# One attention norm of a gated-scan and Hadamard-FFN kernel moved earlier and sent through memory

## The chip, the cores and the metric

The kernel runs on one core of a Trainium2 chip. The core has five engines that work beside each other, each from its own queue in order: TensorE (PE in the profile, with PEld for its weight loads), VectorE (DVE), ScalarE (ACT), GpSimd (POOL) and SyncE (SP), which here only issues DMAs. POOL issues DMAs too: its stores stand in its queue between its few arithmetic instructions. The metric is the device time of one execution in microseconds; the median of the runs shown is compared. Everything is computed in float32.

## The reference

Four sequences of 512 rows and 512 columns go through an attention layer and a feed-forward layer, each behind a layer norm, with a residual sum of the normalized output:

```python
x = x + _layernorm(_L0_attn_ref(_layernorm(x), Wi, Wf, Wg, Wo, gnorm_w))
x = x + _layernorm(_L0_ffn_ref(_layernorm(x), W1, W2, W3))

# attention: i, f, g = x Wi^T, x Wf^T, x Wg^T
gate = sigmoid(f); v = silu(i) * (1 - gate)
o_t = gate_t * o_(t-1) + v_t                 # a scan over the 512 rows
o = o * rsqrt(mean(o * o) + EPS) * gnorm_w * g * sigmoid(g)
out = o Wo^T

# feed-forward: hidden = silu(x W1^T) * (x W3^T), 2048 wide
out = fwht(hidden) W2^T                      # Walsh-Hadamard transform of each row
```

The Hadamard transform of `hidden` is done on W2 instead, once, at the start of the kernel.

## The kernel before

**Products.** Each large product is done with seven block products in place of eight. Both sides are cut into 2x2 blocks; VectorE makes four combinations of each side (`combine_left`, `combine_right`: S1 to S4 and T1 to T4), and `seven` (L445) runs the products in the order P1, P2, P6, P5, P7, P3, P4. P1, P6 and P5 are first copied out of PSUM by ScalarE (L470), P2, P7 and P3 are added by VectorE (L468), and P4 closes with a copy or a sum. Two products share one PSUM bank (X: P1, P6, P7, P4), so P6 may start when the copy of P1 has read the bank, P7 when that of P6 has, and P4 when the sum of P7 has.

**Units.** An attention layer of a sequence b is three units of seven products: `attn_unit(b, 0)` and `attn_unit(b, 1)` give two halves of i and f and, behind P4, the gates and the scan; `attn_unit(b, 2)` gives g and the gated output `og`. The scan of a unit is cut in two: the first half directly behind the gates (`scan(0)`, L523), the second during the next unit, behind its P7 (`second`, put into `beside` at step 4). `attn_out(b)` is the product with Wo: its seven steps are put into the list `fill` and taken out one by one between the products of the following units. The feed-forward layer has eight units for each sequence and four partial output products.

**The norm and the transpose.** A unit's right side is the normalized x, transposed. `normalize_tiles` (L251) takes the statistics of two row tiles on VectorE, the power -1/2 on POOL (L244), and applies scale and bias on ScalarE (L289), tile by tile. From there two ways lead on. For sequences 0 and 1 of the attention layer (`ON_TENSOR`, L249), `transposes` uses TensorE with an identity into four PSUM banks (`pt`, L386), and VectorE and ScalarE copy the result out. For all others ScalarE writes the columns in a folded order, POOL stores the tile to memory (L298), SP loads it back in 32-row pieces (`load_fold`, L418, eight DMAs of 128 KB), and VectorE's 32x32 stream transpose finishes it (`transpose_fold`, L436, two steps of four instructions and then `combine_right`).

**Order.** The orders of TensorE and SP are those of the program text. VectorE, ScalarE and POOL are ordered by a planner by priority; `tc.high_priority(offset=...)` moves work forward (URGENT is 400, SOON 200) and `behind(what)` keeps it behind a named instruction, such as the read of P7 of the current unit. `beside[k]` holds work to be made after product k of the next unit. `acts` and `sums` hold small steps of the output norms; `pace` says how many of `sums` are released after P2, P7 and P3. FULL, SLOW and NONE are three such paces.

**Start of the kernel.** In the first 70 us, sequence 0 runs its three attention units; the w2 matrix is transformed between their products (`transform_high` on TensorE, L742, `butterfly_a` and `butterfly_b` on VectorE, L747 to L761, stores by POOL); the combined weights are stored (`kept`, L161) so that later sequences reload them with one DMA each (`again`, L168). The statistics of sequence 1's norm stand behind unit (0,1) on VectorE; the norm is applied in unit (0,2), and the TensorE transposes stand at the end of it. `load_wo` and `prepare_wo` (L697 and L708) load Wo, scale it by gnorm and combine it; both halves are prepared in one step after P2 of unit (0,2). In SP's queue `load_wo` is followed at once by the reloads of wi and wf for unit (1,0).

Of the kernel before, what the change touches and what calls it, by code (L numbers as in the profile page):

```python
# [44 lines left out]
def kernel(  # L45
# [50 lines left out]
    def slot():  # L96
# [8 lines left out]
    pace = {}  # L105
    FULL, SLOW, NONE = (
        {"P2": a, "P7": b, "P3": c} 
        for a, b, c in ((1, 1, 3), (0, 1, 2), (0, 0, 0))
    )
    pace.update(FULL)  # L110

# [28 lines left out]
    def combine_left(t, eng, steps=(0, 1)):  # L140

        if 0 in steps:
            eng.tensor_add(t[:, S1], t[:, A21], t[:, A22])
            eng.tensor_sub(t[:, S2], t[:, S1], t[:, A11])
        if 1 not in steps:
            return
        eng.tensor_sub(t[:, S3], t[:, A11], t[:, A21])
        return eng.tensor_sub(t[:, S4], t[:, A12], t[:, S2])
# [40 lines left out]
    def combine_weights(n=None, steps=(0, 1)):  # L189
        for _ in range(len(uncombined) if n is None else n):  # L190
            key, t = uncombined.pop(0)
            read["combined"] = combine_left(t, nc.vector, steps)
            if 1 in steps:
                kept(key, t)
            else:
                uncombined.append((key, t))
# [33 lines left out]
    def behind(what):  # L230


        return tc.issue_after(read[what].ins)
# [12 lines left out]

    xns, xnd = {}, {}

    ON_TENSOR = ("a", 0), ("a", 1)  # L249

    def normalize_tiles(b, name, i0, n, later=False):  # L251

        if (name, b) not in xns:
            xns[name, b] = work.tile(  # L260
                [P, NT, D], F32, tag="wide", name=f"xn_{name}_{b}", bufs=3
            )
        t = xns[name, b]
        st = small.tile([P, n, 6], F32, tag=f"st{n}", name=f"st_{name}_{b}_{i0}")
        mv = small.tile([P, n, 2], F32, tag=f"mv{n}", name=f"mv_{name}_{b}_{i0}")
        for k in range(n):
            nc.vector.bn_stats(st[:, k, :], xs[b][:, i0 + k, :])
            nc.vector.bn_aggr(mv[:, k, :], st[:, k, :])
        r = inverse_root(mv, EPS, f"{name}_{b}_{i0}")
        nb = small.tile([P, n], F32, tag="nb", name=f"nb_{name}_{b}_{i0}", bufs=8)  # L270

        def bias():

            read["nb"] = nc.vector.scalar_tensor_tensor(
                nb, mv[:, :, 0], -1.0, r, ALU.mult, ALU.mult
            )

        if later != "bias":
            bias()

        def apply(tiles=range(n)):
            if later == "bias":
                bias()
            for k in tiles:
                x_t, to = xs[b][:, i0 + k, :], t[:, i0 + k, :]
                if (name, b) not in ON_TENSOR:
                    x_t = x_t.rearrange("p (i a c) -> p i c a", c=ND, a=32)
                    to = to.rearrange("p (i c a) -> p i c a", c=ND, a=32)
                read["xn"] = nc.scalar.activation(  # L289
                    to, x_t, AF.Identity, bias=nb[:, k : k + 1], scale=r[:, k : k + 1]  # L290
                )
            if (name, b) not in ON_TENSOR:
                if (name, b) not in xnd:
                    xnd[name, b] = scratch.tile(
                        [NT, P, D], F32, tag=f"xn_{name}_{b}", name=f"xnd_{name}_{b}"
                    )
                if tiles[-1] == n - 1:
                    nc.gpsimd.dma_start(  # L298
                        out=xnd[name, b][i0 : i0 + n].rearrange("t p d -> p t d"),
                        in_=t[:, i0 : i0 + n, :],  # L300
                    )

        if later:
            return apply
        apply()
# [193 lines left out]
    def into_left(t, a, b2, c=None):  # L499

        to = t[:, 0:4] if c is None else t[:, 0:4, c]
        nc.vector.tensor_mul(  # L502
            to.rearrange("p (t k) f -> p k t f", t=2),
            a.rearrange("p k (t f) -> p k t f", t=2),
            b2.rearrange("p k (t f) -> p k t f", t=2),
        )
# [4 lines left out]
    def attn_unit(b, u, dense=False):  # L511
        def gates(d):

            v, gate = d[:, 0], d[:, 1]
            nc.scalar.activation(gate, gate, AF.Tanh, scale=0.5)
            nc.scalar.activation(v, v, AF.Silu)
            nc.vector.scalar_tensor_tensor(v, gate, 1.0, v, ALU.subtract, ALU.mult)
            nc.scalar.activation(gate, gate, AF.Identity, bias=half_t, scale=0.5)
            if u == 0:
                os_[b] = work.tile([P, 2, 2, T], F32, tag="o", name=f"o_{b}")  # L520

            def scan(h):
                nc.vector.tensor_tensor_scan(  # L523
                    os_[b][:, u, h, :], gate[:, h, :], v[:, h, :], 0.0, ALU.mult, ALU.add
                )

            def second():
                with behind("P7"):
                    scan(1)

            scan(0)
            beside.setdefault(4, []).append(second)

        def output_gate(d):
            o = os_[b]
            og = work.tile([P, 7, 2, H], F32, tag="og", name=f"og_{b}")
            for m in range(2):
                nc.scalar.activation(d[:, m], d[:, m], AF.Silu)
                into_left(og, o[:, m], d[:, m], m)
            combine_left(og, nc.vector)  # L540
            ogs[b] = og

            def square(m):
                nc.scalar.activation(o[:, m], o[:, m], AF.Square)
                if m:
                    nc.vector.tensor_add(o[:, 0], o[:, 0], o[:, 1])
                    nc.vector.tensor_add(o[:, 0, 0], o[:, 0, 0], o[:, 0, 1])

            acts.insert(1, partial(square, 1))
            acts.appendleft(partial(square, 0))  # L550

        project(
            attn_w.pop((b, u)), xts["a", b], f"a_{b}_{u}", gates if u < 2 else output_gate,
            dense,
        )
# [149 lines left out]
                )  # L705
        return w

    def prepare_wo(w):  # L708
        for c in range(2):
            for k, blocks in enumerate(((B11, B12), (B21, B22))):  # L710
                t = w[c][:, blocks[0] : blocks[1] + 1 : blocks[1] - blocks[0]]
                g = gn_sb[:, 2 * k + c : 2 * k + c + 1]
                nc.vector.tensor_scalar(t, t, g, -1.0, ALU.mult, ALU.mult)
            combine_right(w[c], nc.vector)
            kept(("wo", c), w[c])
# [29 lines left out]
    def butterfly_a(g):  # L745

        x, y = w2_p[2 * g], w2_p[2 * g + 1]  # L747
        nc.vector.tensor_add(x[:, 2], x[:, 0], y[:, 0])
        nc.vector.tensor_sub(y[:, 0], x[:, 0], y[:, 0])
        nc.vector.tensor_add(x[:, 0], x[:, 1], y[:, 1])  # L750
        nc.vector.tensor_sub(y[:, 1], x[:, 1], y[:, 1])
# [109 lines left out]

    fill.extend([second_half] + high(2, NJ))
    attn_unit(0, 0, True)
    with behind("P2"):
        combine_weights(2)
        for g in range(2):
            butterfly_a(g)
            butterfly_b(g)
    attn_unit(0, 1)
    with behind("P3"):  # L870
        with tc.high_priority(offset=URGENT):
            combine_weights(2)
        with tc.high_priority(offset=SOON):
            apply = [normalize_tiles(1, "a", i, 2, True) for i in (0, 2)]
    with behind("P2"):
        butterfly_a(2)
    wo_t[0] = load_wo()
    load_attn_w(1, 0)
    while fill:
        slot()  # L880

    def wo_behind_sum():
        with behind("P2"):
            prepare_wo(wo_t[0])

    def behind_copy(*makes):
        with behind("copy"):
            for make in makes:
                make()

    fill.extend([wo_behind_sum, partial(behind_copy, *apply)] + transposes(1, "a"))
    attn_unit(0, 2)
    load_x(2)
    load_attn_w(1, 1)
# [1 line left out]
    def beside_copies(b, places):  # L896
# [2 lines left out]
            late = [normalize_tiles(b, "a", i, 2, True) for i in (0, 2)]  # L899
        for t, place in enumerate(places):  # L900
            yield place, partial(behind_copy, partial(late[t // 2], range(t % 2, t % 2 + 1)))

    def transpose_beside(b, name, places=((1, "P2"), (4, "P7"), (6, "P3"))):


        def step(make, what):
            with behind(what), tc.high_priority(offset=SOON):
                make()

        for make, (k, what) in zip(transpose_fold(b, name), places):  # L910
            beside.setdefault(k, []).append(partial(step, make, what))

    fill.extend([None] * 3 + attn_out(0))
    attn_unit(1, 0, True)
# [7 lines left out]
    pace.update(SLOW)  # L922
    attn_unit(1, 2)
    pace.update(FULL)
    load_attn_w(2, 1)
    fill.extend([None] * 3 + attn_out(1))
    for k, what, make, g in (
# [7 lines left out]
        transpose_beside(0, "f", ((6, "P3"), (7, "P2"), (8, "P7")))  # L935

    beside.setdefault(2, []).append(fold_beside)
    attn_unit(2, 1, True)
    load_ffn_w(0, 0)
    load_low(0)  # L940
# [2 lines left out]
    pace.update(NONE)  # L943
    attn_unit(2, 2)
    pace.update(SLOW)
    with behind("P7"), tc.high_priority(offset=SOON):
        combine_weights()

    LOW = {1: (0, "combined", 0), 3: (1, "P2", 2), 5: (2, "P2", 2), 6: (3, "P2", 2)}

# [92 lines left out]
```

## Time and profile before

| | |
|---|---|
| median of 3 runs | 817.80 us (817.74 to 818.98) |
| the profiled execution's own time | 817.91 us |
| its span, first to last instruction | 816.1 us |
| TensorE busy | 802.0 us (98%), mean granted clock 0.995 |
| VectorE, ScalarE, POOL busy | 492.7 (60%), 265.6 (33%), 68.0 (8%) us |
| DMA | 160.62 MB, mean 197 GB/s |

A time line gives the start in microseconds from the span's start, the duration, the engine, the line of the source, the operation, the tiles (out<-in) and shapes, and in brackets the idle time of that engine before it and what ended it. `d_a` is the projection of an attention unit, `d_f` that of a feed-forward unit, `xt` the transposed right side, `og` the gated output, `y` the attention's output. A list of waits gives who waited for whom, the total, the count and the longest. DMA lines give size and time from issue to landing; SPq and POOLq are the queues that issue.

### The profile page before, as it was taken

The numbers are of one execution on the slowest core, as the hardware profiler recorded it, in microseconds if no ns is written. First come the engines' busy times: TensorE is split into PE (matmuls) and PEld (weight loads), VectorE is DVE, ScalarE is ACT, GpSimd is POOL, SyncE is SP. The second block draws the span as 40 slices with busy tenths as digits, with TensorE's granted clock in tenths as the row PEclk, the third lists the DMA queues.
The fourth block names the chain that finished last, engine by engine and source line by source line (L and its number), as shares of the span: only waits on it lengthen the run. The fifth ranks groups of instructions, "written<-read, shape, count | busy, mean of one in ns | idle before, by whom it ended". The sixth has DMA issues, their size and how long they took to land.

```text
span 816.1 us, 9850 instructions
## 1 busy us (share of the span) xinstructions
PE 802.0 (98%) x3704; PEld 698.6 (86%) x3704; DVE 492.7 (60%) x1002; ACT 265.6 (33%) x376; POOL 68.0 (8%) x105
## 2 busy tenths in 40 slices
PE   9999999999999999999999999999999999999995
PEld 7788878888888888888888888888888888888884
DVE  6998599799778874455335448645433534544345
ACT  4564654444442221123311233323432111331111
POOL 2120102011211000011000000101000000100000
PEclk9999999999999999999999999999999999999998
DMA  9995355676777883444654354726373442534201
GB/s 332 408 352 211 113 217 209 179 259 213 282 274 288 277 300 139 185 162 192 248 157 173 139 163 162 270 94 233 115 249 130 186 181 91 204 156 188 88 4 51
DMA packets 66415, 160.62 MB, mean 197 GB/s; under 512 B 4800, under 2 KB 40256, under 8 KB 66368
## 3 DMA queue, kind: packets, MB, share of 16 engines
q1 hardware_dynamic: 57168, 115.69, 40.6%
q0 software_dynamic: 8480, 43.00, 13.3%
q10 hardware_dynamic: 720, 1.31, 0.4%
q8 instruction: 29, 0.48, 0.2%
q14 instruction: 18, 0.15, 0.1%
HBM read 115.94 MB, written 44.04 MB: 196 GB/s over the span
## 4 chain that ended last, share of the span: by engine, by line
PE 94%; DVE 4%; ACT 0%; issue 0%; POOL 0%; POOLq 0%; DVEq 0%; ACTq 0%
PE X_f L487 27%; PE Z_f L487 14%; PE X_po L645 13%; PE X_a L487 9%; PE Z_po L645 7%; PE Y_f L487 6%; PE Z_a L487 4%; PE X_y L587 3%; PE Y_po L645 3%; PE Y_a L487 2%; PE Z_y L587 2%; PE h L742 2%; PE Y_y L587 1%; PE warm L818 1%; DVE o L523 0%; PE pt_a L386 0%
## 5 line engine op out<-in xcount | busy, mean ns | idle before, releaser
L487 PE MATMUL X_f<-xt_f,w 128*128 128x256 f32 x1024 | 242.1, 379 | 1.2 <-ACT d_f L470 1.2
L487 PEld LDWEIGHTS X_f<-xt_f,w 128*128 128x128 f32 x1024 | 194.2, 190 | 28.2 <-ACT d_f L470 2.0
L470 ACT COPY d_f<-X_f 128x512 f32<-128x512 f32 x96 | 56.3, 586 | 331.7 <-PE X_f L487 294.2
L645 PE MATMUL X_po<-w,ht 128*128 128x256 f32 x512 | 120.9, 379 | 0.2 <-DVE f L468 0.2
L487 PE MATMUL Z_f<-xt_f,w 128*128 128x256 f32 x512 | 121.0, 379 | 0.0
L645 PEld LDWEIGHTS X_po<-w,ht 128*128 128x128 f32 x512 | 97.2, 190 | 13.8 <-DVE f L468 0.6
L487 PEld LDWEIGHTS Z_f<-xt_f,w 128*128 128x128 f32 x512 | 97.3, 190 | 13.2
L468 DVE TENSOR_TENSOR f<-X_po,f 128x512 f32<-128x512 f32 x51 | 35.1, 688 | 93.8 <-PE X_po L645 93.7
L502 DVE TENSOR_TENSOR ht<-d_f 128x1024 f32<-128x1024 f32 x32 | 39.2, 1224 | 61.7 <-ACT d_f L621 46.9
L645 PE MATMUL Z_po<-w,ht 128*128 128x256 f32 x256 | 60.5, 379 | 0.0
L487 PE MATMUL Y_f<-xt_f,w 128*128 128x256 f32 x256 | 60.5, 379 | 0.0
L487 PEld LDWEIGHTS Y_f<-xt_f,w 128*128 128x128 f32 x256 | 48.6, 190 | 6.6
L645 PEld LDWEIGHTS Z_po<-w,ht 128*128 128x128 f32 x256 | 48.6, 190 | 6.6
L468 DVE TENSOR_TENSOR d_f<-X_f,d_f 128x512 f32<-128x512 f32 x32 | 22.1, 690 | 50.9 <-PE X_f L487 43.3
L244 POOL TENSOR_TENSOR rs_f<-rs_f,power 128x2 f32<-128x2 f32 x16 | 14.4, 900 | 401.1 <-DVE nm_f L345 347.1
L470 ACT COPY d_a<-X_a 128x512 f32<-128x512 f32 x36 | 21.1, 585 | 69.8 <-PE X_a L487 67.3
L487 PE MATMUL X_a<-xt_a,wi 128*128 128x256 f32 x128 | 33.3, 382 | 1.1 <-ACT d_a L470 1.0
L621 ACT ACTIVATE d_f<-d_f 128x1024 f32<-128x1024 f32 x32 | 33.8, 1057 | 1.0
L487 PE MATMUL X_a<-xt_a,wf 128*128 128x256 f32 x128 | 32.8, 379 | 0.0
L468 DVE TENSOR_TENSOR d_f<-Z_f,d_f 128x512 f32<-128x512 f32 x32 | 21.9, 685 | 16.4 <-PE Z_f L487 16.4
L487 PEld LDWEIGHTS X_a<-xt_a,wi 128*128 128x128 f32 x128 | 23.9, 190 | 8.9 <-issue 2.9
L468 DVE TENSOR_TENSOR f<-Z_po,f 128x512 f32<-128x512 f32 x28 | 19.3, 688 | 20.1 <-PE Z_po L645 20.1
(161 smaller groups left out, 1023.9 us busy)
## 6 DMA issues: line engine op xcount, KB each, us to landing
w<-s_w SPq DMA_DIRECT2D x72, 896.0 KB, 6.0
s_w<-w POOLq DMA_DIRECT2D x24, 896.0 KB, 6.4
w<-in_W_dram SPq DMA_DIRECT2D x32, 256.0 KB, 5.9
wi<-s_wi SPq DMA_DIRECT2D x6, 896.0 KB, 9.5
wf<-s_wf SPq DMA_DIRECT2D x6, 896.0 KB, 8.1
wg<-s_wg SPq DMA_DIRECT2D x6, 896.0 KB, 5.5
w_h<-w2p POOLq DMA_DIRECT2D x8, 512.0 KB, 7.6
xnd_f<-xn_f POOLq DMA_DIRECT2D x8, 512.0 KB, 5.1
```

Source lines behind the costliest of these rows:

```text
L244: read["power"] = nc.gpsimd.tensor_tensor(r, r, power_t[:, 0:n], ALU.pow)
L468: read[what] = nc.vector.tensor_add(to, ps[which], to)
L470: read["copy"] = nc.scalar.copy(to, ps[which])
L487: nc.tensor.matmul(ps[:, n, :], w[:, a, c, :], xt[:, bb, c, :], start=first and n == 0 and c == 0, stop=c == 1, skip_group_check=True,)
L502: nc.vector.tensor_mul(to.rearrange("p (t k) f -> p k t f", t=2), a.rearrange("p k (t f) -> p k t f", t=2), b2.rearrange("p k (t f) -> p k ...
L587: nc.tensor.matmul(ps[:, t, :], og[:, a, c, ts(t, P)], w[c][:, bb, :], start=first and t == 0 and c == 0, stop=c == 1, skip_group_check=True,)
L621: nc.scalar.activation(d[:, 0], d[:, 0], AF.Silu)
L645: nc.tensor.matmul(ps[:, t, :], hts[b, m][:, a, ts(t, P)], w[m][:, W2[bb], :], start=first and t == 0 and m == ms[0], stop=m == ms[-1], sk ...
L742: nc.tensor.matmul(p, h_sb, t[:, k, :], start=True, stop=True)
L818: nc.tensor.matmul(p, ident, ident, start=True, stop=True)
```

## The change

Six things are edited together:

1. `ON_TENSOR` keeps sequence 0 alone. Sequence 1's attention norm takes the other way: folded by ScalarE, stored by POOL, loaded by SP, transposed by VectorE.
2. Its statistics stand behind P3 of unit (0,0) at SOON, and its applications beside products 0 and 3 of unit (0,1). The fold loads stand in SP's queue between `load_wo` and the reloads for unit (1,0). The transposes stand beside products 4, 5 and 6 of unit (0,2), behind P7, P3 and P3.
3. Wo is prepared in two steps, its first half behind P2 and its second behind P3 of unit (0,2).
4. Every second scan gets the priority URGENT.
5. For sequence 1, the products and combinations of `og` get the priority SOON.
6. SLOW releases one step after P3, not two; unit (2,0) releases none after P2; the weights of the first feed-forward unit are combined in two steps with priorities of their own.

```diff
-        for a, b, c in ((1, 1, 3), (0, 1, 2), (0, 0, 0))
+        for a, b, c in ((1, 1, 3), (0, 1, 1), (0, 0, 0))
...
-    ON_TENSOR = ("a", 0), ("a", 1)
+    ON_TENSOR = (("a", 0),)
...
-                with behind("P7"):
+                with behind("P7"), tc.high_priority(offset=URGENT):
                     scan(1)
...
-                into_left(og, o[:, m], d[:, m], m)
-            combine_left(og, nc.vector)
+                with tc.high_priority(offset=SOON if b == 1 else 0):
+                    into_left(og, o[:, m], d[:, m], m)
+            with tc.high_priority(offset=SOON if b == 1 else 0):
+                combine_left(og, nc.vector)
...
-    def prepare_wo(w):
-        for c in range(2):
+    def prepare_wo(w, cs):
+        for c in cs:
...
     attn_unit(0, 0, True)
+    with behind("P3"), tc.high_priority(offset=SOON):
+        apply = [normalize_tiles(1, "a", i, 2, True) for i in (0, 2)]
     with behind("P2"):
         combine_weights(2)
         for g in range(2):
             butterfly_a(g)
             butterfly_b(g)
+    for k, make in zip((0, 3), apply):
+        beside.setdefault(k, []).append(partial(behind_copy, make))
     attn_unit(0, 1)
-    with behind("P3"):
-        with tc.high_priority(offset=URGENT):
-            combine_weights(2)
-        with tc.high_priority(offset=SOON):
-            apply = [normalize_tiles(1, "a", i, 2, True) for i in (0, 2)]
+    with behind("P3"), tc.high_priority(offset=URGENT):
+        combine_weights(2)
     with behind("P2"):
         butterfly_a(2)
     wo_t[0] = load_wo()
+    load_fold(1, "a")
     load_attn_w(1, 0)
     while fill:
         slot()
...
-    fill.extend([wo_behind_sum, partial(behind_copy, *apply)] + transposes(1, "a"))
+    transpose_beside(1, "a", ((4, "P7"), (5, "P3"), (6, "P3")))
+    beside.setdefault(1, []).append(partial(wo_behind_sum, "P2", 0))
+    beside.setdefault(6, []).append(partial(wo_behind_sum, "P3", 1))
     attn_unit(0, 2)
...
     pace.update(FULL)
+    pace["P2"] = 0
     load_attn_w(2, 1)
...
     beside.setdefault(2, []).append(fold_beside)
+    pace.update(FULL)
     attn_unit(2, 1, True)
...
-    with behind("P7"), tc.high_priority(offset=SOON):
-        combine_weights()
+    with behind("P7"):
+        with tc.high_priority(offset=SOON + 100):
+            combine_weights(2, (0,))
+        with tc.high_priority(offset=SOON):
+            combine_weights(2, (1,))
```

`transpose_beside` existed and is moved up; for each step of `transpose_fold` it puts the step beside product k, behind the named read and at SOON.

## The prediction

> **What bounds the kernel now.** I read the busy shares first, then TensorE's own waits, then its timeline at each wait, then what the other engines did just before, and last the DMA queues of the first 70 us.
>
> ```profile
> PE 802.0 (98%) x3704; PEld 698.6 (86%) x3704; DVE 492.7 (60%) x1002; ACT 265.6 (33%) x376; POOL 68.0 (8%) x105
> ```
>
> TensorE is the bound. A change pays by taking work off TensorE or by closing a gap in it, and it costs by opening one. The gaps, in TensorE's timeline:
>
> ```profile
> 114.90 1.13 PE L487 MATMUL X_a<-xt_a,wi 128*128 128x256 f32 x4 [0.97 <-ACT d_a L470]
> 119.87 1.56 PE L587 MATMUL X_y<-wo,og 128*128 128x256 f32 x6 [0.82 <-DVE og L502]
> 165.93 1.99 PE L487 MATMUL X_f<-xt_f,w 128*128 128x256 f32 x8 [0.43 <-ACT d_f L470]
> 506.23 1.99 PE L487 MATMUL X_f<-xt_f,w 128*128 128x256 f32 x8 [0.72 <-ACT d_f L470]
> ```
>
> Three of them end with ScalarE's copy of a new unit's first product. VectorE's and ScalarE's timelines show what that copy waited for: it writes the buffer that a second scan still reads.
>
> ```profile
> 112.96 1.22 DVE L523 TENSOR_TENSOR_SCAN o<-d_a 128x512 f32<-128x512 f32 x1
> 114.27 0.59 ACT L470 COPY d_a<-X_a 128x512 f32<-128x512 f32 x1 [1.13 <-DVE o L523]
> ```
>
> The transposes of sequence 1, in the chain of work that ended last:
>
> ```profile
> 57.22 0.95 PE pt_a L386 x8
> 59.90 0.95 PE pt_a L386 x8
> ```
>
> Next, what one norm application costs ScalarE: four plain ones (sequence 1, the x4 row), and two that write the column-folded order (sequence 2, the x2 row).
>
> ```profile
> 54.29 2.93 ACT L289 ACTIVATE xn_a<-x,nb_a,rs_a 128x512 f32<-128x512 f32 x4
> 83.50 2.52 ACT L289 ACTIVATE xn_a<-x,nb_a,rs_a 128x512 f32<-128x512 f32 x2
> ```
>
> That is 0.73 against 1.26 us a tile. Then the DMA side, in stretches (columns: length, busy time of TensorE, its weight loads, VectorE, ScalarE and POOL, granted clock, DMA share, GB/s) and, in single windows, three reloads that wait in SP's queue (last number: issue to landing):
>
> ```profile
> 20.00:43.00 23.00, 23.00 (x93) 17.38 (x93) 20.96 (x35) 11.12 (x16) 3.95 (x6) 1.00 1.03 400
> 50.00:56.00 6.00, 6.00 (x30) 5.28 (x29) 5.51 (x14) 3.13 (x6) 0.99 (x2) 1.00 1.00 414
> 56.00:62.00 6.00, 6.00 (x37) 5.52 (x36) 5.16 (x13) 3.90 (x7) 0.53 (x1) 1.00 1.04 420
> 69.00:76.00 7.00, 7.00 (x34) 6.15 (x34) 6.97 (x15) 0.59 (x1) 0.71 (x1) 1.00 0.06 26
> ```
>
> ```profile
> wi<-s_wi SPq DMA_DIRECT2D x1, 896.0 KB, 7.7
> ...
> wf<-s_wf SPq DMA_DIRECT2D x1, 896.0 KB, 11.2
> ...
> wi<-s_wi SPq DMA_DIRECT2D x1, 896.0 KB, 19.2
> ```
>
> They were issued at 43.07, 43.55 and 47.36. The engines that move data are full until 69 us, and VectorE is nearly so (20.96 of 23). So the round trip that is added lands where two of its three carriers have no slack.
>
> **The change, part by part** (times are the profiled run's; a product takes TensorE 1.73 us).
>
> *Transposes leave TensorE.* Two groups go: 2 x 0.95 = **-1.90**. VectorE trades 6 PSUM copies (0.74 + 1.42 = 2.16) for 8 stream transposes (two groups of 4 at 1.41, so 2.8); ScalarE loses 2 copies (0.65).
>
> The Trainium skill, "VectorE: DVE Perf Modes", § Rules for kernel authors, advises TensorE for a 128x128 transpose whose result may go to PSUM, which speaks against this move. It counts one operation; here TensorE is 98% busy and VectorE 60%. By the rule the 1.90 would be no gain and the sum below would end 1.9 later; I go by the rows.
>
> *The norm moves into unit (0,1).* VectorE's 2.8 us of statistics (45.25 to 48.0 today) enter at 27.0, right behind P3's addition (26.44), before the second half of the w2 butterflies. ScalarE's four tiles now cost 4 x 1.26 and stand between the copies. I walk ScalarE's new order: copy of P1 to 33.5, tile to 34.8, gate (L518) to 35.8, tile to 37.05, w2 copy to 37.55, copy of P6 to 38.15. P7 wants that bank at 38.09: 0.1 late. POOL's two power steps (2.42 together) come before the first tile is due, between w2 stores. Then copy of P5, two tiles to 41.05, w2 copy to 41.65; VectorE's butterfly waits for it and holds P7's addition behind it, to 42.9, while P4 wants to start at 42.40 + 0.1: 0.5 late. VectorE then combines wg until 47.9 (45.25 today), the gate step and ScalarE's L518 follow to 50.5, the copy of P1 of unit (0,2) to 51.1, and its P6, due at 50.15 + 0.6, is 0.35 late. Together **+1.0**. Ends: 0 if the two engines slip less, 2.8 if every added VectorE microsecond came through.
>
> *Wait in SP's queue.* Three things now stand ahead of the reloads of wi and wf for unit (1,0): wo's second half, which waits for a w2 store that VectorE finishes 4.6 us later (POOL issues it at about 39.4 instead of 34.81, so with the 4.1 us of the store of 139.19 it lands at 43.5 instead of 41.7), and eight fold loads, each half waiting for its norm store. POOL's own queue has these stores among the w2 stores, the second at 41.2; the first waits for ScalarE until 37.1, and the w2 store behind it is ready only at 38.9, so nothing is held up. With 3.1 us to land (the later norm store of sequence 2 took that) plus some crowding, the folds are issued from 45.0, 0.45 each, and wi and wf at 48.8 and 49.3 instead of 43.07 and 43.55. Behind SP's wait stand x_2 and the second reload pair, needed only at 70 us and later.
>
> When does wf land? From 47.0 on the engines must move the folds (sequence 2's first half, alone from 89.4 to 93.5, took 44.6% of 4.1 us = 1.83; 3.7 for both), the two wg stores (50 to 56: 62.3% of 6 us for 1.57 MB, so 2.1 each, 4.3), wi and wf (2.1 each by that rate, 2.64 by the lone reload of 78 to 82.3) and one wo store (2.1). The sum is 14.3 to 15.4, so wf lands at 61.4 to 62.4. Bounds by rows: the same reload's own 11.2 gives 60.5; the longest, 19.2, gives 68.5. I take **62.0**, near the first, since the added load is known and small.
>
> *What TensorE makes of it.* P1 of unit (1,0) starts at 60.69 - 1.90 + 1.0 = 59.8 and wants wf 0.86 later, at 60.65: **+1.35**. P2 then starts at 62.86 (62.42 today) and P6 at 64.59, with the 0.29 gap that stands before it today (64.14 to 64.43) gone: **-0.29**. T2 is no obstacle then: VectorE adds P7 at about 56.6, scans (1.13), transposes 8 (2.7) around P3's addition (0.6), and has T1, one wo scaling and T2 (1.6) done by 63.3; og by 66.8, wanted at 68.0. Without the reload's wait this chain would allow P6 at 63.4.
>
> *Second scans behind P7, urgent.* Walked for the three gaps. Unit (1,2): X addition to 108.0, scan to 109.1, T2 at 113.15, ScalarE's silu pair to 113.1 and the copy to 113.7; P6 wants 113.77. At 165: scan to 160.4, T2 164.0, copy 165.25 for 165.33. At 506: scan to 500.45, T2 504.3, copy 505.2 for 505.35. All just fit: **-0.97, -0.43, -0.72**, with 0 to +0.3 each as the doubt, since the silu pair is late next. I take +0.2 for the three.
>
> *og of sequence 1 at SOON.* Its two products come straight after T3, done at 115.8 for a need at 117.2: **-0.82**. The residual and the statistics that stood ahead are late instead: xn_f_0's first half goes to ScalarE about 5 us later.
>
> *Paces, wo in two steps, weights in two steps, longer queue entries.* 0 each. Cover: fold_f_0's second half lands at 147.3 and is transposed at 154.4, so 7 us; if that were used up VectorE would wait in front of P6's T2. Wo's second half is scaled before the products that read it. Bounds 0 to +0.5.
>
> Sum: -1.90 + 1.0 + 1.35 - 0.29 - 0.97 - 0.82 - 0.43 - 0.72 + 0.2 = **-2.6**. The profiled execution took 817.91 (span 816.1, 1.8 around it), 0.11 above the median 817.80: 815.3 for it, **815.2** for the median.
>
> **The rivals.**
>
> *The reloads come in time* (wf before 60.6). For: 11.2 us was measured with the engines full. Against: 3.7 us of folds are now ahead in the same queue. P6 of (1,0) at 63.4, so 1.0 earlier than today; with the gaps, 817.8 - 1.0 - 2.94 + 0.2 = 814.1.
>
> *The start of sequence 1 gives the gaps back.* Crowding or the strided norms cost 2 us more than I count (wf at 64): P6 at 66.6, 2.2 later than today, less 2.74: 817.3, no measurable change. For: the 43 to 50 us stretch moved only 261 GB/s with a share of 0.91.
>
> *Slower: wf's landing becomes the bound.* With the 19.2 us row it lands at 68.5, P6 starts at 71.1, 6.7 late: 817.8 + 6.7 - 2.74 = 821.8. It decides from a landing at 66.2 on (0.2% slower). Against: that reload stood behind 1 MB of x and two stores.
>
> *The change does not do what it says*: silu, not the scan, holds the copy. Then 0.97, 0.43 and 0.72 stay: 815.2 + 2.1 = 817.3. Against: the copy's recorded release is the scan.
>
> **How the numbers follow.** Chances: forecast 0.52 (own range 814.4 to 816.1), in time 0.2, gaps given back 0.13, silu 0.05, slower 0.10. A difference under 0.2% (1.6 us) can't be told from none, so faster means below 816.2: 0.50 + 0.20 = 0.70; within: 0.02 + 0.13 + 0.05 = 0.20; slower 0.10. The range runs from a little under the second case to a little above the third, 813.5 to 817.9, which leaves out the slow case and a tail.
>
> **What would show it.** Right: TensorE without a transpose group at 57 and 60, no gap near 113, 118, 165 and 505, one gap of about 1 to 1.5 us at the first wf product of unit (1,0) released by a DMA, and small ones near 38, 42 and 50. Wrong: a gap before that unit released by VectorE's transposes (folds late), a gap there above 4 us, or gaps that return at 113 or 505 released by the same copy.

## The result, and the profile after

The changed kernel takes 823.02 us (median of 4 runs, 822.37 to 824.89) where the kernel before, run beside it, takes 818.0 us (817.74 to 818.98): a ratio of 1.0058, 95% interval 1.0045 to 1.0070. It is slower by 5.0 us; 815.2 was predicted, and 817.9 was the upper end of the range. The profiled execution took 823.37 us with a span of 821.6 (before: 817.91 and 816.1), so the traces account for 5.5 us.

The page's busy line of the changed kernel:

```profile
PE 803.2 (98%) x3688; PEld 696.8 (85%) x3688; DVE 492.9 (60%) x1004; ACT 266.1 (32%) x374; POOL 68.0 (8%) x107
```

TensorE has 16 instructions less and is busy 1.2 us longer, although 1.9 us of transposes left it. That is a first sign that some products ran slowly. TensorE's list of waits (what it waited for, us in total, times, the longest) shows two new ones on top:

```profile
PE X_a L487 <- DVE xt_a L154: 4.0, 1, 4.0
PE X_y L589 <- ACT y L470: 2.2, 1, 2.2
...
PE X_a L487 <- DMA wf<-s_wf: 0.5, 1, 0.5
```

**The first is the start of unit (1,0).** TensorE's timeline there:

```profile
58.21 1.89 PE L487 MATMUL X_a<-xt_a,wg 128*128 128x256 f32 x8
64.10 2.04 PE L487 MATMUL X_a<-xt_a,wi 128*128 128x256 f32 x4 [4.00 <-DVE xt_a L154]
66.64 2.08 PE L487 MATMUL X_a<-xt_a,wf 128*128 128x256 f32 x4 [0.50 <-DMA wf<-s_wf]
68.51 1.54 PE L487 MATMUL Y_a<-xt_a,wi 128*128 128x256 f32 x4
69.89 1.03 PE L487 MATMUL Y_a<-xt_a,wf 128*128 128x256 f32 x4
70.75 1.03 PE L487 MATMUL X_a<-xt_a,wi 128*128 128x256 f32 x4
```

The 4.00 us wait is put down to VectorE's combination (L154), but the blocks that the first product needs were transposed by 61.8; wi lands at 63.96 and wf at 66.60, issued at 53.93 and 54.65.

```profile
59.74 2.05 DVE L436 STREAM_TRANSPOSE xt_a<-fold_a 128x256 f32<-128x256 f32 x6
63.28 0.69 DVE L154 TENSOR_TENSOR xt_a<-xt_a 128x512 f32<-128x512 f32 x1
```

It is the reload that is late: in two of the runs below (x_2 behind the next reloads, and the stores held in POOL's queue) the same wait, of 3.51 and 3.80 us, carries wi's own name. The second thing to see is the duration: four products take 2.04 and 2.08 us behind the wait and 1.03 further on. The stretches say why (columns: length, busy time of TensorE, its weight loads, VectorE, ScalarE, POOL, then the granted clock, the share of the data engines and GB/s):

```profile
46.00:60.00 14.00, 14.00 (x61) 11.13 (x59) 10.76 (x23) 6.28 (x10) 1.64 (x3) 1.00 1.02 337
60.00:64.00 4.00, 0.10 (x1) 0.00 (x0) 4.00 (x11) 2.59 (x3) 0.00 (x0) 0.84 1.01 423
64.00:68.00 4.00, 3.40 (x7) 2.35 (x8) 3.83 (x5) 0.00 (x0) 0.00 (x0) 0.50 1.05 415
```

The granted clock falls to half at 62.72 us and stays there for 6.83 us, to 69.55. And the engines that move data are full (1.01 to 1.05) all the way.

P6 of unit (1,0), the product that the prediction followed, starts at 70.75 instead of 64.43: 6.32 later. The parts, from the two timelines: 0.55 was there at 27 us already (this run's first loads came later); -1.90 for the transposes; +0.76 for what units (0,1) and (0,2) slip; -0.29 for a gap that stood before P6; +5.68 of waiting for wi and wf, as it would be at full clock (4.00, and 1.68 that the wf products would wait); +1.52 for the half clock, counted from the first wf product (66.64 to 70.75 is 4.11, three times 0.86 is 2.59).

**The second is new, at 132.74.** TensorE stands 2.19 us before y's second product for ScalarE's copy of the first. ScalarE's and VectorE's timelines:

```profile
124.16 1.06 ACT L546 ACTIVATE o<-o 128x1024 f32<-128x1024 f32 x1
130.90 1.31 ACT L289 ACTIVATE xn_f<-x,nb_f,rs_f 128x512 f32<-128x512 f32 x1 [5.68 <-DVE nb_f L274]
132.12 0.56 ACT L470 COPY y<-X_y 128x512 f32<-128x512 f32 x1
```

```profile
119.72 2.35 DVE L502 TENSOR_TENSOR og<-o,d_a 128x1024 f32<-128x1024 f32 x2
...
125.61 1.27 DVE L267 BATCH_NORM_STATS2 st_f<-x 128x6 f32<-128x512 f32 x2
...
130.71 0.16 DVE L274 SCALAR_TENSOR_TENSOR nb_f<-mv_f,rs_f 128x2 f32<-128x2 f32 x1 [0.58 <-POOL rs_f L244]
```

In the kernel before, the statistics came ahead of og:

```profile
114.09 1.26 DVE L267 BATCH_NORM_STATS2 st_f<-x 128x6 f32<-128x512 f32 x2
...
116.72 1.22 DVE L502 TENSOR_TENSOR og<-o,d_a 128x1024 f32<-128x1024 f32 x1
```

Now og comes first (119.72), the statistics that make nb_f follow at 125.61, and ScalarE, which takes its queue in order, stands 5.68 us at the xn_f tile. The copy of y's first product is behind it, and was wanted near 125.4.

What was promised did happen: no transposes at 57 and 60, and the gaps of 0.97, 0.82, 0.43 and 0.72 near 115, 120, 166 and 506 are gone. 6.32 - 2.94 + 2.19 = 5.57, the 5.5 of the spans.

### The profile page after: what moved, and what is told of

It is laid out like the page before. It is cut to its first block, busy times and chain, and to the rows that moved or that the text cites. A ratio compares the mean times of both kernels' runs of the same rounds, so it can differ in the third digit from the quotient of the medians.

```text
span 821.6 us, 9836 instructions
## 1 busy us (share of the span) xinstructions
PE 803.2 (98%) x3688; PEld 696.8 (85%) x3688; DVE 492.9 (60%) x1004; ACT 266.1 (32%) x374; POOL 68.0 (8%) x107
## 4 chain that ended last, share of the span: by engine, by line
PE 87%; DVE 5%; DMA 4%; ACT 1%; SPq 1%; issue 1%; POOLq 0%; POOL 0%; DVEq 0%
PE X_f L487 26%; PE X_po L647 13%; PE Z_f L487 13%; PE X_a L487 7%; PE Z_po L647 7%; PE Y_f L487 7%; PE X_y L589 3%; PE Y_po L647 3%; PE Z_a L487 3%; PE Y_a L487 2%; DMA wg<-in_Wg_dram 2%; PE Z_y L589 2%; DMA wf<-s_wf 1%; DMA w2p<-in_W_dram 1%; SPq L180 1%
## 5 line engine op out<-in xcount | busy, mean ns | idle before, releaser
L487 PE MATMUL Y_f<-xt_f,w 128*128 128x256 f32 x256 | 60.5, 379 | 0.0
L647 PE MATMUL Z_po<-w,ht 128*128 128x256 f32 x256 | 60.5, 379 | 0.0
L589 PE MATMUL X_y<-wo,og 128*128 128x256 f32 x128 | 30.3, 380 | 2.2 <-ACT y L470 2.2
```

Of the source, the lines that this page charges most:

```text
L487: nc.tensor.matmul(ps[:, n, :], w[:, a, c, :], xt[:, bb, c, :], start=first and n == 0 and c == 0, stop=c == 1, skip_group_check=True,)
L589: nc.tensor.matmul(ps[:, t, :], og[:, a, c, ts(t, P)], w[c][:, bb, :], start=first and t == 0 and c == 0, stop=c == 1, skip_group_check=True,)
L647: nc.tensor.matmul(ps[:, t, :], hts[b, m][:, a, ts(t, P)], w[m][:, W2[bb], :], start=first and t == 0 and m == ms[0], stop=m == ms[-1], sk ...
```

## The experiments

For the start of unit (1,0) the theory is that of the sum: the data engines are full from 46.7 to 66.6 us, and wf lands when all that is in them ahead of it is done. Its rival is the order: SP issued the reloads late, behind the folds. For the gap at 132.74 the theory is og's priority, the rival the changed paces. The kernel before had a median of 818.07, 818.42, 818.49 and 818.20 us in the four groups; ratios are to it, with 95% intervals.

### The urgent second scan alone

```diff
--- before.py
             def second():
-                with behind("P7"):
+                with behind("P7"), tc.high_priority(offset=URGENT):
                     scan(1)
```

> The kernel before, with the second scan behind P7's addition as urgent and nothing else. Theory (the recorded step on the second scans holds, and is independent of the rest of the change): the gaps of 0.97, 0.43 and 0.72 us before the copies of new units close, the 0.82 gap at og stays; 818.0 - 2.1 + 0.2 = 815.9 us (815.7 to 816.2). Rival (the silu pair, not the scan, holds the copy): 817.8 to 818.0, the gap near 113 us still there.

816.88 us (11 runs), ratio 0.9990 (0.9981 to 0.9999). The gaps of 0.97, 0.43 and 0.72 closed, but only 1.2 us came of it. TensorE's timeline:

```profile
117.97 0.67 PE L587 MATMUL X_y<-wo,og 128*128 128x256 f32 x2 [0.70 <-DVE og L502]
119.76 1.56 PE L587 MATMUL X_y<-wo,og 128*128 128x256 f32 x6 [1.11 <-DVE og L502]
```

The 0.97 was given back five microseconds on: og's second wait ends at 119.76, in the kernel before at 119.87. That chain did not move, so TensorE only reached it sooner. What remains is 0.43 + 0.72 = 1.15, the gain measured. The silu rival is out; the recorded sum of -0.97 and -0.82 as two independent terms holds only where both are done.

### The scan and og at SOON

```diff
--- before.py
+                with behind("P7"), tc.high_priority(offset=URGENT):
                     scan(1)
...
+                with tc.high_priority(offset=SOON if b == 1 else 0):
+                    into_left(og, o[:, m], d[:, m], m)
+            with tc.high_priority(offset=SOON if b == 1 else 0):
+                combine_left(og, nc.vector)
```

> The kernel before, with the urgent second scan and og of sequence 1 at SOON. Recorded step (og at SOON costs nothing behind it): all four gaps gone, 818.0 - 2.94 = 815.1 us. Theory from the trace after (og pushes the residual and the statistics of xn_f back on VectorE, the first xn_f tile then holds ScalarE's queue with the copy of y's first product behind it): a new TensorE gap of about 2 us in front of a product X_y<-wo,og near 128 us, so 818.0 - 2.94 + 2.2 = 817.3 us (816.8 to 817.8), 1.2 to 1.5 slower than the urgent scans alone.

818.67 us (11 runs, 817.32 to 820.16), ratio 1.0002 (0.9992 to 1.0012). The four gaps are gone and the new one is there:

```profile
126.17 2.77 PE L589 MATMUL X_y<-wo,og 128*128 128x256 f32 x8 [2.19 <-ACT y L470]
128.73 1.91 PE L487 MATMUL X_a<-xt_a,wi 128*128 128x256 f32 x4
```

So the 2.19 us belong to og's priority and not to the norm's move. They cost more than expected: in this profile the clock was at half from 127.25 to 130.66, and eight products took 2.77 us instead of 1.89. Three of the runs took 817.32 or 817.33, what was expected without that.

### og late in the changed kernel

The reverse: the changed kernel with those og lines as in the kernel before.

```diff
--- after.py
-                with tc.high_priority(offset=SOON if b == 1 else 0):
-                    into_left(og, o[:, m], d[:, m], m)
-            with tc.high_priority(offset=SOON if b == 1 else 0):
-                combine_left(og, nc.vector)
+                into_left(og, o[:, m], d[:, m], m)
+            combine_left(og, nc.vector)
```

> The changed kernel, with og of sequence 1 back at its ordinary priority. Theory (og at SOON made the 2.19 us gap at 132.74): that gap is gone; the waits for og come back, at the 0.70 + 1.11 us that the urgent scans alone left them: 823.0 - 2.19 + 1.8 = 822.6 us (821.6 to 823.0). Rival (the paces, or P2 taken out of them, made the gap): it stays, and og's waits come on top, 823.8 to 824.8 us.

820.93 us (5 runs), ratio 1.0034 (1.0021 to 1.0048). The 2.19 us gap is gone, with the changed paces still in, so these did not make it. og's waits came back with 0.44 instead of the 1.8 expected, so the result lies under the stated range. In its trace P6 of unit (1,0) also starts 1.7 us sooner (69.05): 0.65 was there at 27 us, wf landed at 65.47, and the half clock lasted 3.41 us instead of 6.83.

### The tile behind the copy

Scans and og on the kernel before, and ScalarE's list of spare work in another order: both squares and one empty place stand ahead of the first xn_f tile.

```diff
--- the scan and og at SOON
-            acts.insert(1, partial(square, 1))
+            if b == 1:
+                acts.extendleft((lambda: None, partial(square, 1)))
+            else:
+                acts.insert(1, partial(square, 1))
             acts.appendleft(partial(square, 0))
```

> The kernel before, with the urgent second scan, og of sequence 1 at SOON, and both squares of o_1 and an empty place ahead of the first xn_f tile in the list that ScalarE's spare places are filled from, so that the copy of y's first product stands before that tile in ScalarE's queue. Theory (the tile in front of the copy made the 2.19 us gap, nothing else does): no gap over 0.2 us between 110 and 510 us, 818.0 - 2.94 = 815.1 us (814.8 to 815.8). Rival (the tile, still waiting for the late statistics, holds the next copy instead): a gap of 1 to 2 us one product later, 816.3 to 817.5 us.

814.89 us (5 runs, 814.76 to 815.36), ratio 0.9958 (0.9945 to 0.9970). In ScalarE's timeline the copy now goes first, and the tile waits where nobody is behind it in time:

```profile
119.40 0.59 ACT L470 COPY y<-X_y 128x512 f32<-128x512 f32 x1 [1.14 <-PE X_y L592]
124.90 1.33 ACT L289 ACTIVATE xn_f<-x,nb_f,rs_f 128x512 f32<-128x512 f32 x1 [4.92 <-DVE nb_f L274]
126.30 0.59 ACT L470 COPY y<-X_y 128x512 f32<-128x512 f32 x1
```

TensorE has no wait over 0.2 us left behind its start. This is the mechanism of the second wait, shown by removing it, and the four gaps together are worth what the prediction said.

### The norm's move alone

The changed kernel with scan, og and paces as before; what remains is the norm of sequence 1 in unit (0,1), its folds, the transposes on VectorE, wo in two steps and the weights of the first feed-forward unit in two steps.

```diff
--- after.py
-        for a, b, c in ((1, 1, 3), (0, 1, 1), (0, 0, 0))
+        for a, b, c in ((1, 1, 3), (0, 1, 2), (0, 0, 0))
...
-                with behind("P7"), tc.high_priority(offset=URGENT):
+                with behind("P7"):
                     scan(1)
...
-    pace["P2"] = 0
...
-    pace.update(FULL)
     attn_unit(2, 1, True)
```

> Only the norm of sequence 1 in unit (0,1), its folds, the transposes on VectorE and wo in two steps; scans, og and paces as before. Recorded steps: -1.90 + 1.0 + 1.35 - 0.29 = +0.16, so 818.2 us. Theory from the trace after (P6 of unit (1,0) at 70.75 instead of 64.43 us, 0.55 of it from the start of that run): 818.0 + 5.8 = 823.8 us (823 to 825), with the gaps near 113, 118, 165 and 505 us as in the kernel before.

824.75 us (4 runs), ratio 1.0079 (1.0065 to 1.0093), as the reading of the trace had it and 6.5 above the recorded steps. Its start of unit (1,0):

```profile
61.15 1.10 PE L487 MATMUL X_a<-xt_a,wi 128*128 128x256 f32 x4 [1.90 <-DMA wi<-s_wi]
64.55 2.08 PE L487 MATMUL X_a<-xt_a,wf 128*128 128x256 f32 x4 [2.29 <-DMA wf<-s_wf]
```

Here both waits carry the reloads' names. This part alone makes the kernel slower: P6 of unit (1,0) starts 5.4 us later than in the kernel before (69.81). Another 1.0 of the 6.5 us between the spans comes at 172 us, where the wait of 0.43 has grown to 1.44. By VectorE's order it is the price of the two-step weights: eight of their combinations now stand ahead of the second scan, where five did in the kernel before, and ScalarE's copy waits for the scan. No run tests them alone.

```profile
169.97 0.42 DVE L148 TENSOR_TENSOR w<-w 128x256 f32<-128x256 f32 x1
170.30 1.22 DVE L523 TENSOR_TENSOR_SCAN o<-d_a 128x512 f32<-128x512 f32 x1
```

### Reloads ahead of the folds

```diff
--- after.py
-    load_fold(1, "a")
     load_attn_w(1, 0)
+    load_fold(1, "a")
```

> The changed kernel, with wi and wf of unit (1,0) loaded ahead of the eight fold loads in SP's queue. Theory of the order (the reloads were late because SP waited with them behind the folds): wf lands near 58 us, the first product of unit (1,0) waits for the folds and VectorE's transposes instead, which land by about 61; gap under 2 us in place of 4.0 and 0.5, time 819 to 820.5 us. Theory of the sum (the engines that move data are full from 46.7 to 66.6 us, so what is taken from wf is given to the folds): the folds land at 63 to 65, the transposes follow, the gap is 4 to 6 us again, time 822 to 825 us.

829.86 us (4 runs), ratio 1.0142 (1.0128 to 1.0155). wf, issued at 46.86, lands at 58.34, 8.3 us sooner; the last fold lands at 67.58 instead of 60.26, 7.3 later. TensorE waits twice for VectorE's transposes:

```profile
65.75 2.07 PE L487 MATMUL X_a<-xt_a,wi 128*128 128x256 f32 x4 [6.51 <-DVE xt_a L436]
...
75.43 1.10 PE L487 MATMUL X_a<-xt_a,wi 128*128 128x256 f32 x4 [4.05 <-DVE xt_a L153]
```

wf's landing followed its issue, but what one gains the other loses, so the order in SP's queue only chooses which of the two is late. It came out worse than the theory of the sum said (822 to 825): the last fold was later than its 63 to 65, and the second wait was not foreseen.

### x_2 behind the next reloads

```diff
--- after.py
-    load_x(2)
     load_attn_w(1, 1)
+    load_x(2)
```

> The changed kernel, with the four loads of x_2 behind the second pair of reloads in SP's queue. They moved 496 of their 512 packets before wf was in, 2.66 us of engine time that the recorded sum did not count. Theory of the sum: wf lands up to 2.7 us sooner, at 63.9 to 65, the gap before unit (1,0) shrinks from 4.0 to 1.5 to 2.5 us and the half clock behind it may go with it, time 818.5 to 821 us. Theory of the order (the late issue at 54.65 us alone sets the landing): wf at 66 to 67, time 822.5 to 823.5 us.

823.37 us (5 runs), ratio 1.0064 (1.0051 to 1.0076): no change, and wf lands at 66.10. The expectation counted wrong: of the packets of x_2's size that moved before wf landed, 128 are wo's, so x_2 had moved 368 of 512, 1.9 us of engine time. In this run 94 packets of the next reload moved instead, 1.8 us. So what stands behind wf in the queue moves while part of wf is still missing, whichever load it is. That x_2 in particular delays wf is out; but the run put as much work in its place, so whether wf would land sooner with nothing behind it is not shown. That some of the 16 data engines finish their share of wf earlier than others would explain it; it is only argued, for the records do not tell the engine.

### The stores of wg and wo held back

First in POOL's own queue, behind the copy of unit (1,0)'s first product in the planner's order (a store marked late goes into the list held_stores):

```diff
--- after.py
-        combine_weights(2)
+        combine_weights(2, late=True)
...
-            kept(("wo", c), w[c])
+            kept(("wo", c), w[c], c == 0)
...
+    def store_held():
+        with behind("copy"):
+            while held_stores:
+                kept(*held_stores.pop(0))
+    beside.setdefault(0, []).append(store_held)
     fill.extend([None] * 3 + attn_out(0))
     attn_unit(1, 0, True)
```

> The changed kernel, with three stores of POOL's queue (the two of wg and the first of wo) held until the copy of the first product of unit (1,0). They take 4.7 + 2.2 us of the engines that move data between 46.7 and 66.6 us. Theory of the sum: the folds land by about 54, wi and wf by 57 to 61, the gap of 4.0 + 0.5 us is under 1 us and the clock stays whole; P6 of unit (1,0), at 70.75 us, starts at 64 to 65.5, held by VectorE's T2 if by anything; 823.0 - 5.5 to 6.5 = 816.5 to 817.5 us, with the 2.19 us gap at y still in it. Rival (VectorE, not the data, is what the unit waits for next): the gap moves to the transposes and T2 and only half comes back, 819 to 821 us.

823.01 us (5 runs), ratio 1.0054 (1.0041 to 1.0067). The stores started at 47.01, 48.01 and 54.42, no later than in the changed kernel (47.65, 48.65 and 55.06): an order in the planner is no wait on the chip, and POOL, with nothing ahead of them that waits, issued them at once. This run tells nothing of the theory and repeats the changed kernel. Then from ScalarE's queue, where the copy stands ahead of them:

```diff
--- the stores held in POOL's queue
-                kept(*held_stores.pop(0))
+                kept(*held_stores.pop(0), eng=nc.scalar)
```

> The changed kernel, with the two stores of wg and the first store of wo issued from ScalarE's queue, in which they stand behind the copy of the first product of unit (1,0); in that order they cannot start before it. (In the run that held them in POOL's queue they had nothing to wait for and started at 47.01, 48.01 and 54.42 us as before, so that run repeated the changed kernel.) Theory of the sum: 6.9 us of engine time less ahead of wf; the folds land by about 55, wf by 58 to 61, the gap before unit (1,0) is under 1 us, the clock stays whole, P6 starts at 64 to 65.5: 823.0 - 5.5 to 6.5 = 816.5 to 817.5 us. Rival (the order of SP's queue alone): wf lands where it did, 65.5 to 66.6, and the time stays at 823 us. Rival (VectorE is the next to be waited for): gap moves to T2, 819 to 821 us.

816.82 us (12 runs), ratio 0.9975 (0.9967 to 0.9984): 6.2 us less than the changed kernel, from three stores. The folds land by 55.04, wf, issued at 52.07, at 62.59:

```profile
59.49 1.03 PE L492 MATMUL X_a<-xt_a,wi 128*128 128x256 f32 x4
62.63 1.13 PE L492 MATMUL X_a<-xt_a,wf 128*128 128x256 f32 x4 [2.12 <-DMA wf<-s_wf]
```

The granted clock stays whole. wf is later than the 58 to 61 that was expected, and the wait 2.12 instead of under 1, but P6 starts at 65.33, within the stated bounds, since the clock costs nothing. The theory of the sum holds in its direction and in the time: taking 6.9 us of other traffic out of the same engines moved wf and the folds by 4 and 5 us. Its landing for wf was 1.6 us too early at the least.

### Stores held and the tile behind the copy

Both edits on the changed kernel.

```diff
--- the stores issued from ScalarE's queue
-            acts.insert(1, partial(square, 1))
+            if b == 1:
+                acts.extendleft((lambda: None, partial(square, 1)))
+            else:
+                acts.insert(1, partial(square, 1))
```

> As the run with the stores held, with the first xn_f tile also put behind the copy of y's first product. Theory: the 2.19 us gap goes as well, 816.5 to 817.5 less 2.2 = 814.3 to 815.3 us, level with or better than 814.9 us of the kernel before with the scans, og and the tile's place. Rival (the held stores crowd out x_2 and the reloads of units (1,1) and (1,2)): new gaps at 75 to 95 us, 816 to 819 us.

813.70 us (5 runs, 812.79 to 814.97), ratio 0.9943 (0.9931 to 0.9954). TensorE's waits behind its start:

```profile
PE X_a L492 <- DMA wf<-s_wf: 1.6, 1, 1.6
...
PE X_po L655 <- DVE f L473: 0.2, 1, 0.2
```

It beats the kernel before by 0.57%, and the changed one, by the medians of two groups, by 1.1%. Against the 0.42% of the kernel with scans, og and tile only, the intervals overlap: whether the transposes on VectorE are worth having is not settled. In the traces P6 of unit (1,0) starts at 64.51 here and at 64.67 there, so the wait for wf has used up most of the 1.9 us.

### TensorE kept busy in the wait

Idle products of the identity with itself, ahead of unit (1,0); 32 of them first, then 16.

```diff
--- after.py
+    with behind("P3"):
+        warm_up(32)
     fill.extend([None] * 3 + attn_out(0))
     attn_unit(1, 0, True)
```

> The changed kernel, with 32 products of the identity with itself (128x128, about 0.11 us each) put into TensorE's wait before unit (1,0); their result is used by nothing. Theory (the clock that was granted fell to half because TensorE stood for 4 us, and this costs 1.5 us on top of the wait): the granted clock stays at 1.0 through 60 to 72 us, the four products with wi take 1.03 instead of 2.04 us, P6 starts at about 69.2 instead of 70.75 us: 821.5 us (820.8 to 822). Rival (the products are slow for another reason, such as the full data engines): 823 us, products at 2.0 us.

824.37 us (5 runs), ratio 1.0069 (1.0057 to 1.0081). The clock stayed whole and the four products took 1.03 us, but each idle product took 0.22 us and not 0.11, so they ended at 66.69, 1.6 us after wf had landed. From 27 us to P6 (70.15) it is 43.30 us, 0.20 less than in the changed kernel: the filler itself used up the gain. That the profiled execution is longer than the changed kernel's has another reason, for in it the clock fell at y's wait:

```profile
132.15 3.67 PE L589 MATMUL X_y<-wo,og 128*128 128x256 f32 x8 [2.21 <-ACT y L470]
```

```diff
--- 32 idle products
-        warm_up(32)
+        warm_up(16)
```

> The changed kernel, with 16 idle products of the identity in TensorE's wait before unit (1,0). The run with 32 of them took 7.14 us for them, 0.22 each, so it ended 1.6 us after wf had landed; 16 take 3.6 us and end before wi lands. Theory (the half clock behind the wait costs time of its own): granted clock 1.0 through 60 to 72 us, and from the first product with wf to P6 2.6 to 2.7 us instead of 4.11, so 823.0 - 1.5 = 821.5 us (820.5 to 822). Rival (the half clock hides in the wait for wf): 2.6 to 2.7 us as well, but the first product with wf starts no earlier than 66.6 and the time stays at 822.5 to 823.5 us.

821.99 us (6 runs), ratio 1.0038 (1.0026 to 1.0050). The stretches and TensorE's timeline of that run:

```profile
60.00:64.00 4.00, 3.15 (x29) 2.96 (x27) 2.27 (x7) 2.20 (x3) 0.00 (x0) 1.00 1.01 422
64.00:68.00 4.00, 2.38 (x10) 1.83 (x11) 4.00 (x7) 0.11 (x1) 0.00 (x0) 1.00 1.03 411
```

```profile
66.72 1.13 PE L487 MATMUL X_a<-xt_a,wf 128*128 128x256 f32 x4 [0.94 <-DMA wf<-s_wf]
...
69.41 1.03 PE L487 MATMUL X_a<-xt_a,wi 128*128 128x256 f32 x4
```

wf lands at the same time as in the changed kernel (66.67), and from its first product to P6 it is 2.69 us instead of 4.11. So the half clock was a cost of its own, 1.4 us in the traces and 1.0 in the medians; the intervals of the two ratios overlap a little, so it is the traces that carry this.

## Why the prediction was wrong

**Wait in SP's queue: the step that failed.** It took wf's landing at 62.0; it landed at 66.60, inside the recorded bounds (60.5 to 68.5) and past the 66.2 from which the slower rival decides. That rival is what happened, and 0.10 was too little for it. That its 821.8 is close to the time measured is partly luck: it came from a landing at 68.5, and had neither the half clock nor y's wait in it.

The issue was 5.3 us late (54.65, not 49.3): 1.7 because SP, ahead of the folds, waited for a w2 store that landed at 45.37 and not at 43.5 (issued at 40.50 instead of about 39.4, and 4.9 us on its way instead of 4.1); 3.4 because SP did not pass a fold every 0.45 us, for the eight took 7.12; and 0.2 between wi and wf.

```profile
46.02 0.60 SPq L704 DMA_DIRECT2D wo<-in_Wo_dram  x1
46.72 7.12 SPq L418 DMA_DIRECT2D fold_a<-xnd_a  x8
53.93 0.61 SPq L168 DMA_DIRECT2D wi<-s_wi  x1
54.65 0.54 SPq L168 DMA_DIRECT2D wf<-s_wf  x1
```

From its issue to its landing wf then took 11.95 us, no more than the 12.7 of the step, and in all fourteen traces it lands 9.2 to 12.0 us behind its issue. So the delay is already there at the issue, and the issue is late because of the traffic: with the three stores held, SP passes the folds in 4.44 us and issues wf 2.6 us sooner.

```profile
47.02 4.44 SPq L423 DMA_DIRECT2D fold_a<-xnd_a  x8
51.57 0.39 SPq L173 DMA_DIRECT2D wi<-s_wi  x1
52.07 0.36 SPq L173 DMA_DIRECT2D wf<-s_wf  x1
```

What holds SP between two folds is not shown. The work in the engines is the same delay, counted in another way. The trace's packet records between 46.7 and 66.6 give it: folds 3.69 us of all 16 engines (3.7 in the sum), the wg stores 4.69 (4.3), wi and wf 5.15 (4.2 to 5.3), the wo store 2.19 (2.1). These terms were right. Left out were the rest of wo's loads, 1.81, which the step took to be in by then (they landed at 51.14 and 51.74 instead of the 44.83 and 45.52 of before), the tail of the norm store, 0.51, and the 1.9 of x_2 that moves while wf is unfinished. Together 20.0 us, and 46.7 + 20.0 is the landing, as it must be where the engines are full all the way; what the records add is whose work it was. So the term was mis-sized by 4.2 us of work that its list did not name, of which the 1.9 of x_2 may not have delayed wf: the step moved three users of a full resource and summed only from the middle of their queue.

**What TensorE makes of it.** +1.35 was predicted and 5.68 + 1.52 measured. The 1.52 has no step: the prediction read clock 1.00 in every stretch of the trace before, where no wait was longer than 1 us, and did not ask what a wait of 4 us does to it.

**og of sequence 1 at SOON.** The step said that the residual and statistics would be late and xn_f_0's first half would reach ScalarE about 5 us later, and priced that at 0. The delay was right (5.68 us of idle) and the price wrong, because nothing asked what was queued behind that tile: the copy of y's first product. -0.82 became +1.4.

**What held.** The transposes gave -1.90. Units (0,1) and (0,2) slipped 0.76 for a predicted 1.0, with 0.18 of it as a wait before P4 of unit (0,1). The three gaps closed by the scan and og's own did close, and the run with the tile behind the copy measured -3.5 us for the four where -2.94 + 0.2 was the sum. VectorE's T2 was in time. Paces and the two-step weights cost nothing that the trace of the changed kernel shows; the 1.0 us that the two-step weights cost in the norm-only run is covered there by the urgent scans. The advice of the Trainium skill, "VectorE: DVE Perf Modes", § Rules for kernel authors, to use TensorE for a 128x128 transpose was not what decided: VectorE's transposes were done 2.2 us before wi landed.

The misses are 4.33 + 1.52 + 2.19 = 8.0 us, less 0.24 of slip and 0.2 of doubt; with 0.55 from the start of the run this is the distance from -2.6 to +5.5.

## What to carry to other kernels

Where the data engines are full, as here, a landing is set by the sum of everything that is in them, from whatever queue; look for the traffic that nobody waits for and hold that back with a real wait, for reordering the rest only moves the delay. When something is given priority, name the first instruction that it pushes back, and then what stands behind that one in an in-order queue. A gap of TensorE that is to be closed is worth only the distance to the next wait whose own chain does not move.

## What was not expected of the hardware

The granted clock has two values here, 1.0 and 0.5, and the stretches at 0.5 between 20 and 800 us last 3.41, 6.83 or 10.24 us, multiples of one step. Waits of 3.5 to 4.0 us before unit (1,0) brought it down in every profile that has one (stretches of 6.83 in the changed kernel, 3.41 with og late, 10.24 with x_2 later), at a price of 0.95 to 2.7 us from the first wf product to P6. A wait of 2.2 us at y's second product brought it down in 2 of the 8 profiles that have it, so the same wait costs 2.2 us or, with the products slowed behind it, about 4.

The traces tell the two cases apart. The changes of the clock lie on a grid of 3.41 us steps. Laid on that grid, the fourteen traces show a fall at the end of every step at full clock in which TensorE stood for 2.04 us or more in sum (23 steps, with the ends of the kernels), and of none in which it stood for 1.99 or less. In the two profiles in which y's wait brought the clock down, the whole wait lay within one step (123.84 to 127.25 and 128.76 to 132.17); in the other six two steps shared it, 0.44 and 1.75 us in the changed kernel. The Trainium skill, "TensorE: Matmul & The Clock Gate", § Part 1: The HAM clock gate, describes a free-running window of 3.4 us and two clock states, which these stretches agree with; it puts the fall after an idle window of about 3.4 us, and here 2.0 us of standing within one step was enough.

The four loads of x_2, issued after wf on the same queue, had moved 368 of their 512 packets before wf was complete. And POOL's stores (7168-byte packets of about 290 ns), which nobody was waiting for then, held up the folds (2048 packets of 512 bytes), which landed by 55.0 with the stores held and by 60.3 without: between 46.7 and 60.3 us they took 4.9 us of the engines' time against the folds' 3.7, and while the wg stores moved, from 48 to 56, only 237 to 363 fold packets moved in each 2 us, then 810 in the next 2 us, with four packets of the stores. The Trainium skill, "DMA: Bandwidth & Descriptors", § Queues, rings and completion order, says that an engine goes round its queues packet by packet, which would fit; the turns themselves no record here shows.
